# A two-step graph layer on one Trainium2 core: second step with sums put ahead of the mask, gathers issued singly, a finished tile's end moved, and small operations moved between engines

## The chip, the core and the metric

The kernel runs on one core of one Trainium2 chip. The core has TensorE (PE in the profile, its weight loads are PEld), VectorE (DVE), ScalarE (ACT), GpSimd (POOL) and SyncE (SP)[...] and 16 DMA engines. The metric is the device time of one execution, in microseconds (us); lower is better.

## The reference, cut to what matters

There are N = 3327 nodes with 256 features, padded to 26 tiles of 128 rows. `adj` is sparse: a row has about five entries, the diagonal among them.

```python
h = relu(layernorm(x))
R = (adj + I) / rowsum(adj + I)
Xf = Xa = h;  Z = 0
for n in (0, 1):
    q = Xa @ W1.T @ W2.T;  k = Xa @ W3.T              # 64 wide
    probs = softmax(q @ k.T)                          # 3327 x 3327
    A = probs, cut in each row to the fewest largest entries
        whose sum reaches 0.9, then divided by the row's sum
    Xf = R @ Xf
    Xa = A @ Xa
    Z = Z + Xf @ U1[n].T + Xa @ U2[n].T
out = x + layernorm(h + Z) * ln_g + ln_b
```

No row is sorted. A threshold is guessed for each row from passes of Relu and Sign over the exponentials; then the largest entries below the guess are found exactly, and the cut is placed among them. Had a guess failed, a flag would start a slow search at the end.

## The kernel before, in words

One program works through 26 tiles of 128 rows twice, `step` 0 and `step` 1. A tile's row block `e` is 128 x 3328 numbers in SBUF; step 1 has six such buffers, two of which lie in the former `x0` (the profile then writes `x` where it means such a block).

**What happens to one tile of step 1**, by generator, with its lines:

- `weights` (L580): query product (`pq`, L522), then products with the keys into PSUM (`pl`, L598) and the exponential into `e` (ACT, L602 to L608).
- `measured_twice` (L666): eight pieces. A row of small ACT operations (L618 to L673) makes a first guess; then a Relu pass over the whole block and a Sign pass (both `ja`, L631). Small operations on VectorE (L682, L683), ACT (L684 to L686) and GpSimd (L687 to L689) make a better guess; then a second Sign pass. L694 to L709 (GpSimd), L696, L697 (VectorE) and L699 to L711 (ACT) make the final guess, used by VectorE (L713, L714).
- `settle` (L722): VectorE writes `w`, the entries below the guess (L728), takes the 8 largest of each of 20 segments (L733, 20 MAX8), then the 48 largest of those (L740, L742, six rounds), finds the cut (L747 to L752), and masks `e` in place while it sums it (L762; the first and the last tile do it in two parts, L759). GpSimd multiplies two 48-wide rows (`cum`, L765) for a proof that VectorE ends (L769).
- `Sums` (L798): `turn` transposes a group of four 128 x 128 blocks of the masked `e` on TensorE (`pt`, L811), and ACT copies them out (`eT`, L813); `sum` multiplies them with `xw`, adding into PSUM `pa` (L825). A tile has seven groups. There are two `pt` buffers, three `eT` buffers and one `pa` buffer.
- `spread` (L1073): the sparse product, six 128-wide products (`pr`, L911) of the packed adjacency `ac` with gathered rows `xg`, and `s` on VectorE (L1086). `refetch` (L1092) loads `ac` and issues five gathers of 128 rows on GpSimd (L903), two buffers deep.
- `finish` (L934): VectorE adds the sums into `s` (L935) and takes mean and variance (L457, L458); GpSimd makes the scale (L464, L465, L943); ACT applies it (L950); GpSimd adds `bet` to the re-read `x` (L945), multiplies by `gam` (L951) and adds the two (L952); SP stores.
- `laws` (L548), once at the start of step 1: statistics of the query rows of tiles 3 to 25, ended by a power of 0.5 and eight more small GpSimd operations (L567 to L574).

**Their order is written out by hand.** Round `i` has seven slots. In each slot the letters of `PLAN[step][k]` let one generator advance by one piece: `m` measures tile i+1 and `n` ends the measuring that began in the round before; `d` settles tile i and `c` ends the settling of tile i-1, its mask (slot 0) and proof among it; `s` is `spread`, `w` and `q` are `weights`, `f` is `finish`, `g` the gathers, `l` the laws, `v` the final proof. `LAST` replaces the plan in the final rounds. Around the letters of a slot a `turn` (before them in step 1) and a `sum` (after them) are set. What is left of a generator runs at the round's end. Dependencies added at the end of the function then hold PE, ACT and VectorE, and in step 1 GpSimd, to this order: an engine that waits in one instruction holds up all that is written behind it.

Slot `k` of round `i` serves group `g = 7(i-1) + k - 4` in step 1, and `turn` runs two groups ahead. So a tile's sums begin in slot 4 of the round after its settling began, and its first transposes stand in slot 2, after its mask.

Of the kernel before, what the change touches and what calls it, by code (L numbers as in the profile page):

```python
# [9 lines left out]
F32 = mybir.dt.float32  # L10
# [334 lines left out]
def guess_graph_layer(ctx, tc, x, adj, w1t, w2t, w3t, u1t, u2t, ln_g, ln_b, out, flag):  # L345
# [60 lines left out]
    half = const.tile([P, 4], F32, tag="half", name="half")  # L406
    for k, c in enumerate((-0.5, 0.5, -1.0, -0.5)):
        G.memset(half[:, k : k + 1], c)
    halves = const.tile([P, NT], F32, tag="halves", name="halves")
    G.memset(halves, 0.5)  # L410
    law = const.tile([P, 7, NT], F32, tag="law", name="law")
    one = const.tile([P, 7], F32, tag="one", name="one")
    for k, c in enumerate((1.0, -1.0, 5.0e-4, SQG[1], SQK[1], math.log(10.0), LNY)):
        G.memset(one[:, k : k + 1], c)
    of_s = const.tile([P, 4], F32, tag="of_s", name="of_s")
    for k, c in enumerate((SQG[0], SQG[2], -SQK[0], -SQK[2])):
# [131 lines left out]
    def laws(ts):  # L548

        at = lambda k, a, b: law[:, k, a:b]  # L550
        few_of = [ts[h::2][n : n + 3] for n in range(0, len(ts), 3) for h in range(2)]
        for few in filter(len, few_of):
            pq = ps_t.tile([P, 4, P], F32, tag="pt", name="pq")
            pm = pq.rearrange("p a b -> p (a b)")[:, : 3 * (2 * DA + 2)].rearrange("p (t n) -> p t n", t=3)
            for k, t in enumerate(few):
                PE.matmul(pm[:, k, :], query_of(t), qm[query_at(t), 1, :], start=True, stop=True)
            wide = scan.tile([P, NP], F32, tag="w", name="wide")
            mq = wide[:, : 3 * (2 * DA + 2)].rearrange("p (t n) -> p t n", t=3)
            V.tensor_copy(mq[:, : len(few)], pm[:, : len(few)])
            V.tensor_copy(law[:, 2, few[0] : few[-1] + 1 : 2], mq[:, : len(few), DA])  # L560
            for k, t in enumerate(few):
                V.scalar_tensor_tensor(mq[:, k, : DA + 1], mq[:, k, : DA + 1], 1.0, mq[:, k, DA + 1 :],
                                       ALU.mult, ALU.mult, accum_out=at(1, t, t + 1))
            yield
        a, b = ts[0], ts[-1] + 1
        s, var, m = (at(k, a, b) for k in range(3))
        G.tensor_tensor(s, var, halves[:, a:b], ALU.pow)  # L567
        for k, c in ((3, SQG[0]), (4, SQG[2]), (5, -SQK[0]), (6, -SQK[2])):
            G.tensor_scalar(at(k, a, b), s, c, 1.0e-4, ALU.mult, ALU.add)
        G.tensor_tensor(at(4, a, b), at(4, a, b), var, ALU.add)  # L570
        G.tensor_tensor(at(4, a, b), at(4, a, b), m, ALU.add)
        G.tensor_scalar(m, m, 0.25, LNY - 0.25 * math.log(0.1 / N), ALU.mult, ALU.add)
        G.tensor_scalar(var, var, 0.125, None, ALU.mult)
        G.tensor_tensor(var, var, m, ALU.add)  # L574
# [91 lines left out]
    def measured_twice(r):  # L666
# [19 lines left out]
        S.activation(col(13), col(6), AF.Copy, scale=col(9))  # L686
        G.tensor_scalar(col(14), col(13), col(9), 0.25, ALU.add, ALU.mult)  # L687
        G.tensor_scalar(col(10), col(13), col(5), 1.0, ALU.mult, ALU.add)
        G.tensor_scalar(col(8), col(4), col(1), -1.0, ALU.mult, ALU.add)  # L689
        yield  # L690
        through(e, AF.Sign, col(13), -1.0, oa[:, 2:3])
        yield
# [8 lines left out]
        S.activation(col(3), d1, AF.Ln, scale=col(1), bias=con(2))  # L701
        S.activation(col(2), col(2), AF.Identity, scale=-1.0, bias=col(3))

        G.tensor_scalar(col(12), col(4), d1, col(1), ALU.subtract, ALU.mult)
        G.tensor_scalar(col(8), col(8), col(12), None, ALU.mult)
        G.tensor_scalar(col(12), col(12), col(12), 1.0e-12, ALU.mult, ALU.add)
        G.tensor_tensor(col(12), col(12), half[:, 2:3], ALU.pow)
        G.tensor_scalar(col(12), col(12), col(8), 0.7, ALU.mult, ALU.max)
        G.tensor_scalar(col(11), col(12), 1.5, col(11), ALU.min, ALU.mult)  # L709
        yield  # L710
# [11 lines left out]
    def settle(step, t, r):  # L722
# [38 lines left out]
        else:  # L761
            V.scalar_tensor_tensor(e, e, at(1), e, ALU.is_ge, ALU.mult, accum_out=ra)  # L762
        V.reciprocal(ra, ra)
        if step:
            G.tensor_tensor(cum[:, :n], dr[:, :n], b, ALU.mult)  # L765
        yield
        if not step:
            V.tensor_tensor(cum[:, :n], dr[:, :n], b, ALU.mult)
        V.tensor_reduce(at(2), cum[:, :n], AX.X, ALU.max)  # L769


# [103 lines left out]
    def gathered(t):  # L875
        oh = ohs.pop(t)
        ls, n = lists[:, t, :], LIST - DIRECT
        po = ps_t.tile([P, 4, P], F32, tag="pt", name="po")
        PE.matmul(po[:, 0, : n + 1], oh, ls[:, DIRECT:], start=True, stop=True)
        lo = small.tile([P, n], F32, tag="lo", name="lo", bufs=2)  # L880
        S.copy(lo, po[:, 0, :n])
        nth = small.tile([P, 1], F32, tag="nth", name="nth")
        S.activation(nth, po[:, 0, n : n + 1], AF.Identity, scale=-1.0, bias=part)
        yield
        of = small.tile([P, LIST], F32, tag="of", name="of", bufs=2)
        V.scalar_tensor_tensor(of[:, :n], place[:, :n], nth, lo, ALU.is_equal, ALU.mult, accum_out=nth)
        G.tensor_scalar(index[:, t, DIRECT:], nth, -1.0, float(NONE), ALU.mult, ALU.add)
        ac = adjp.tile([P, KT, P], F32, tag="ac", name="ac", bufs=2)
        nc.sync.dma_start(ac[:, KT - 1, :], adj[t, :, t, :])
        acs[t] = ac  # L890
        G.tensor_tensor(ac[:, KT - 1, :], ac[:, KT - 1, :], ident, ALU.add)
        rows = adj.rearrange("t p j r -> (t p j) r")
        for k in range(KT - 1):
            G.indirect_dma_start(out=ac[:, k, :], out_offset=None, in_=rows,  # L894
                                 in_offset=bass.IndirectOffsetOnAxis(ap=index[:, t, k : k + 1], axis=0),
                                 element_offset=t * P * NT * P)
        xgs[t] = fetched(bx, t, D + 1)

    def fetched(table, t, w):
        xg = adjp.tile([P, KT - 1, D + 1], F32, tag="xg", name="xg", bufs=2)  # L900
        rows = table.rearrange("p j d -> (p j) d")
        for k in range(KT - 1):
            G.indirect_dma_start(out=xg[:, k, :w], out_offset=None, in_=rows,  # L903
                                 in_offset=bass.IndirectOffsetOnAxis(ap=index[:, t, k : k + 1], axis=0))
        return xg


    def diffuse(ac, xg, own, w):
# [25 lines left out]
    def finish(t, y, pa, ra):  # L934
# [7 lines left out]
        nm = small.tile([P, 1], F32, tag="nm", name="nm")  # L942
        G.tensor_scalar(nm, mv[:, 0:1], rstd, -1.0, ALU.mult, ALU.mult)  # L943
        yield
        G.tensor_tensor(xr, xr, bet, ALU.add)  # L945
        if t == NT - 1:
            V.scalar_tensor_tensor(y, y, mv[:, 0:1], gam, ALU.subtract, ALU.mult)
            V.scalar_tensor_tensor(y, y, rstd, xr, ALU.mult, ALU.add)
        else:
            S.activation(y, y, AF.Identity, bias=nm, scale=rstd)  # L950
            G.tensor_tensor(y, y, gam, ALU.mult)  # L951
            G.tensor_tensor(y, y, xr, ALU.add)  # L952
        yield
        h = min(P, N - t * P)
        nc.sync.dma_start(out[t * P : t * P + h], y[:h])

# [135 lines left out]
    def refetch(t):  # L1092
        acs[t] = adjp.tile([P, KT, P], F32, tag="ac", name="ac", bufs=2)
        nc.sync.dma_start(acs[t].rearrange("p k r -> p (k r)"), cx[t])
        xgs[t] = fetched(vx, t, D)
        yield

# [1 line left out]


    PLAN = (("mdsssa", "mcdsssa", "edawwp", "msda", "mpdea", "gdwwq", "emgq"),
            ("llcmss", "lnms", "lwwnfd", "lcmdsssg", "fmswqdf", "llmdf", "lmwfd"))

    LAST = {NT - 1: ("cfss", "cn", "ndd", "sss", "fddddsf", "f", "f"), NT: ("cf", "", "", "", "ff", "fv", "f"),
            NT + 1: ("fv", "f", "", "", "f", "f", "f")}
    LATE = (1, 4)
    trace, begin = nc.cur_bb.bb.instructions, len(nc.cur_bb.bb.instructions)
    work = dict(m=none, d=none, f=none)  # L1110
    later = {}
    ordered = []
    for step in range(2):
        sums = Sums(step, live, xw if step else x0, AHEAD[step])

        for i in range(-1, NT + 2):
# [4 lines left out]
            if step == 1 and i == -1:  # L1121
# [11 lines left out]
                e=first_end(i - 2) if step == 0 and valid(i - 2) else none,  # L1133
                a=itertools.islice(lister, 9 if i else 3) if step == 0 else none,
                p=packed(i + 1) if step == 0 and i >= 0 and valid(i + 1) else none,
                g=none if not valid(i + 2 * step) else refetch(i + 2) if step else gathered(i),
                b=none, q=none, v=proof() if step and i == NT else work.get("v", none),
                l=laws(range(3, NT)) if step and i == -1 else none,
            )
            if i >= 0 and valid(i + 3):  # L1140
                later[step, i + 3] = weights(step, i + 3, live)
# [9 lines left out]
                work["w"] = begun[2]  # L1151
            if step == 0 and i < 1:
                work["b"] = itertools.islice(product, MADE if i else NT)
            if step == 1 and i == -1:
                work["g"] = itertools.chain(refetch(0), refetch(1))
            for k in range(PARTS):
                g = PARTS * (i - 1) + k - LATE[step]
                summing = valid(g // PARTS)
                if summing and step:
                    sums.turn(g, min(i, NT - 1))  # L1160
                for c in "bb" + (LAST.get(i, PLAN[1]) if step else PLAN[0])[k]:
                    next(work[c], None)
                if summing and not step:
                    sums.turn(g, min(i, NT - 1))
                if summing:
                    ended = sums.sum(g)
                    if ended and step == 0:
                        live["r", ended[0]] = ended[1]
                    elif ended:
                        work["f"] = finish(ended[0], live.pop(("f", ended[0])), *ended[1])  # L1170
            if step == 1 and i == -1:
                run(work["m"])
            if step == 0 and i == -1:
                G.memset(es[2][:, N:NP], 0.0)
            for c in "lcnwqsepgb" if step else "cmwqsepgb":
                run(work[c])
            if step == 0 and i == NT:
                moments(1, gsum)
# [52 lines left out]
```

## Time and profile before

| | us |
|---|---|
| median of three runs | 1431.23 (1426.26 to 1432.77) |
| the profiled execution | 1383.37 |
| its span | 1381.4 |
| granted TensorE clock, mean | 0.976 |
| busy: PE, DVE, ACT, POOL | 1271.7, 1207.6, 1109.1, 1022.8 |
| step 0, to about | 740 |
| start of step 1, to the mask of tile 1 | 740 to 811.51 |
| masks of tiles 1 to 23, start to start | 811.51 to 1300.58 |
| mask of tile 24 to the end | 1322.39 to 1381.4 |

The page gives busy time by engine, a strip of 40 slices, the chain of work that ended last, and the costliest groups of instructions; the trace behind it answers for single lines and stretches. Busy time counts the time in which an instruction was at work on an engine, so an engine can be 94% busy and still spend that time on a chain that passes through others. The profiled execution is one run, and it is shorter than the three timed ones.

### The profile page before, as it was taken

The numbers are of one execution on the slowest core, as the hardware profiler recorded it, in microseconds if no ns is written. First come the engines' busy times: TensorE is split into PE (matmuls) and PEld (weight loads), VectorE is DVE, ScalarE is ACT, GpSimd is POOL, SyncE is SP. The second block draws the span as 40 slices with busy tenths as digits, with TensorE's granted clock in tenths as the row PEclk, the third lists the DMA queues.
The fourth block names the chain that finished last, engine by engine and source line by source line (L and its number), as shares of the span: only waits on it lengthen the run. The fifth ranks groups of instructions, "written<-read, shape, count | busy, mean of one in ns | idle before, by whom it ended". The sixth has DMA issues, their size and how long they took to land.

```text
span 1381.4 us, 22149 instructions
## 1 busy us (share of the span) xinstructions
PE 1271.7 (92%) x6495; PEld 977.1 (71%) x6495; DVE 1207.6 (87%) x3595; ACT 1109.1 (80%) x2449; POOL 1022.8 (74%) x1374
## 2 busy tenths in 40 slices
PE   6898999999999999999997389999999999999885
PEld 5545777777877778787775267777776777777674
DVE  6878999999999999999944689999999999999992
ACT  5467888879888888888735689999999999999931
POOL 6225888888888888888843868888888888888832
PEclk9999999999999999999998589999999999999998
DMA  8884453545445453545331211212222221212100
GB/s 293 261 271 125 128 148 109 152 119 152 128 135 141 122 154 106 156 118 149 85 98 50 69 54 55 84 58 81 71 67 82 58 88 54 89 58 81 58 8 22
DMA packets 91202, 149.77 MB, mean 108 GB/s; under 512 B 15265, under 2 KB 58656, under 8 KB 91072
## 3 DMA queue, kind: packets, MB, share of 16 engines
q1 hardware_dynamic: 73616, 105.37, 24.4%
q0 software_dynamic: 16640, 42.69, 11.9%
q8 instruction: 54, 0.88, 0.3%
q14 instruction: 76, 0.62, 0.1%
q10 hardware_dynamic: 816, 0.20, 0.1%
HBM read 120.93 MB, written 27.28 MB: 107 GB/s over the span
## 4 chain that ended last, share of the span: by engine, by line
DVE 40%; PE 24%; ACT 17%; POOL 9%; DMA 4%; issue 4%; SPq 0%; POOLq 0%; DVEq 0%; ACTq 0%
ACT ja L631 11%; PE pa L825 9%; DVE e L762 9%; PE pl L598 5%; DVE cand L733 4%; DVE w L728 4%; DVE fm L847 4%; DVE bb L740 3%; DVE cand L742 3%; PE pt L811 3%; PE pz L988 3%; POOL xg L903 3%; POOL ac L894 2%; DVE x L762 2%; DMA at<-in_adj 2%
## 5 line engine op out<-in xcount | busy, mean ns | idle before, releaser
L825 PE MATMUL pa<-xw,eT 128*128 128x256 f32 x1352 | 330.8, 386 | 6.6 <-DVE s L935 6.5
L631 ACT ACTIVATE ja<-e,g 128x3328 uint8<-128x3328 f32 x106 | 325.8, 3074 | 0.1
L825 PE MATMUL pa<-x,eT 128*128 128x256 f32 x1352 | 323.1, 380 | 0.0
L825 PEld LDWEIGHTS pa<-xw,eT 128*128 128x128 f32 x1352 | 249.4, 191 | 67.9 <-issue 27.1
L825 PEld LDWEIGHTS pa<-x,eT 128*128 128x128 f32 x1352 | 243.7, 191 | 25.8
L733 DVE MAX8 cand<-w 128x8 f32<-128x168 f32 (+1 forms) x1040 | 251.5, 318 | 0.0
L813 ACT COPY eT<-pt 128x512 f32<-128x512 f32 (+1 forms) x364 | 201.9, 556 | 59.3 <-PE pt L811 58.8
L894 POOL DMA_INDIRECT ac<-in_adj,index x130 | 189.7, 1459 | 44.3 <-issue 30.5
L811 PE MATMUL pt<-ident,e 128*128 128x128 f32 x1144 | 180.1, 278 | 43.9 <-DVE e L762 21.9
L811 PEld LDWEIGHTS pt<-ident,e 128*128 128x128 f32 x1144 | 140.5, 144 | 90.2 <-issue 43.3
L903 POOL DMA_INDIRECT xg<-bx,index x130 | 158.0, 1216 | 39.2 <-issue 30.5
L728 DVE SCALAR_TENSOR_TENSOR w<-e,g 128x3328 f32<-128x3328 f32 x44 | 168.5, 3830 | 0.7
L903 POOL DMA_INDIRECT xg<-vx,index x130 | 130.9, 1007 | 45.6 <-issue 33.0
L762 DVE SCALAR_TENSOR_TENSOR e<-e,rec 128x3328 f32<-128x3328 f32 x40 | 153.6, 3840 | 0.6
L911 PE MATMUL pr<-xg,ac 128*128 128x257 f32 (+1 forms) x520 | 139.4, 392 | 11.3 <-DVE s L1086 11.1
L602 ACT ACTIVATE e<-pl 128x832 f32<-128x832 f32 x132 | 112.8, 859 | 30.2 <-PE pl L598 30.1
L911 PEld LDWEIGHTS pr<-xg,ac 128*128 128x128 f32 x520 | 94.0, 195 | 25.0 <-DVE s L1086 11.3
L740 DVE MAX8 bb<-cand 128x8 f32<-128x160 f32 x286 | 92.9, 325 | 6.4
L598 PE MATMUL pl<-after,qT 64*128 64x416 f32 x416 | 96.7, 559 | 0.6 <-ACT qT L527 0.6
L765 POOL TENSOR_TENSOR cum<-dr,bb 128x48 f32<-128x48 f32 x26 | 84.8, 3261 | 15.5 <-DVE rec L752 15.4
L951 POOL TENSOR_TENSOR s<-s,gam 128x256 f32<-128x256 f32 x25 | 92.6, 3703 | 3.2 <-ACT s L950 3.2
L598 PE MATMUL pl<-both,qT 64*128 64x416 f32 x416 | 90.1, 536 | 0.8 <-DVE both L1006 0.8
(257 smaller groups left out, 2200.0 us busy)
## 6 DMA issues: line engine op xcount, KB each, us to landing
at<-in_adj SPq DMA_DIRECT2D x102, 256.0 KB, 3.2
cx<-ac SPq DMA_DIRECT2D x26, 384.0 KB, 2.8
ac<-cx SPq DMA_DIRECT2D x26, 384.0 KB, 3.1
wide<-in_adj SPq DMA_DIRECT2D x10, 832.0 KB, 6.4
e<-in_adj SPq DMA_DIRECT2D x8, 832.0 KB, 5.1
bx<-e SPq DMA_DIRECT2D x26, 128.5 KB, 2.8
own<-bx SPq DMA_DIRECT2D x26, 128.5 KB, 3.2
x<-in_x SPq DMA_DIRECT2D x13, 256.0 KB, 5.4
```

Of the source, the lines that this page charges most:

```text
L598: PE.matmul(pl[:, a, :wd], qT[p, :], keys_of(step, a).rearrange("p a b -> p (a b)")[:, c : c + wd], start=True, stop=True)
L631: S.activation(ja, e, f, bias=guess, scale=sign, accum_out=total)
L728: V.scalar_tensor_tensor(w, e, col(16), e, ALU.is_lt, ALU.mult, accum_out=d2)
L733: V.max(cand[:, 8 * s : 8 * s + 8], w[:, s * SEG : min(NP, (s + 1) * SEG)])
L740: V.max(b8, cand)
L762: V.scalar_tensor_tensor(e, e, at(1), e, ALU.is_ge, ALU.mult, accum_out=ra)
L811: PE.transpose(pt[:, j, :], e[:, (j0 + j) * P : (j0 + j + 1) * P], ident)
L813: S.copy(eT[:, :w, :], pt[:, :w, :])
L825: PE.matmul(self.pa, eT[:, c - 4 * k, :], self.xa[:, j, :], start=c == 0, stop=c == NT - 1)
L894: G.indirect_dma_start(out=ac[:, k, :], out_offset=None, in_=rows, in_offset=bass.IndirectOffsetOnAxis(ap=index[:, t, k : k + 1], axis=0), ...
L903: G.indirect_dma_start(out=xg[:, k, :w], out_offset=None, in_=rows, in_offset=bass.IndirectOffsetOnAxis(ap=index[:, t, k : k + 1], axis=0))
L911: PE.matmul(pr[:, :w], ac[:, k, :], own if k == KT - 1 else xg[:, k, :w], start=k == 0, stop=k == KT - 1)
```

## The change

Step 0 keeps its instructions and their order. Line numbers above are those of the kernel before; the changed one is six to nine lines lower.

- **Sums and transposes.** In step 1 slot 1 runs two `sum`s and slot 2 none; the `turn` of slot 2 does two groups and the one of slot 3 none. Transposes of the first tile begin before its sums do.
- **Gathers.** `fetched` yields after each gather. One chain of all tiles' gathers is drawn on by each `g`; the new `OPEN` plans spread them over the first rounds. From round 4 on five stand together in slot 3.
- **Laws.** The power of 0.5 becomes Ln and Exp on ACT, and the last piece runs at the end of round 0.
- **Guess.** Three small GpSimd operations and a power become one operation and a reciprocal on VectorE; `spread` goes ahead of `measured` in slot 4.
- **Proof.** The 48-wide product goes from GpSimd to VectorE in step 1.
- **End of a tile.** `finish` has four pieces rather than five. The last, with the ACT scaling and the three GpSimd operations, runs in slot 2 of the next round, behind `w`; `bet` is added after `gam` is multiplied.
- **Last rounds.** `LAST` is reordered.

```diff
-        G.tensor_tensor(s, var, halves[:, a:b], ALU.pow)
+        S.activation(s, var, AF.Ln, bias=con(7))
+        S.activation(s, s, AF.Exp, scale=0.5)
...
-        G.tensor_scalar(col(8), col(4), col(1), -1.0, ALU.mult, ALU.add)
+        G.tensor_scalar(col(8), r["Z"], -0.1, col(4), ALU.mult, ALU.add)
...
-        G.tensor_scalar(col(12), col(4), d1, col(1), ALU.subtract, ALU.mult)
-        G.tensor_scalar(col(8), col(8), col(12), None, ALU.mult)
-        G.tensor_scalar(col(12), col(12), col(12), 1.0e-12, ALU.mult, ALU.add)
-        G.tensor_tensor(col(12), col(12), half[:, 2:3], ALU.pow)
+        V.tensor_scalar(col(12), col(4), d1, 1.0e-30, ALU.subtract, ALU.add)
+        V.reciprocal(col(12), col(12))
         G.tensor_scalar(col(12), col(12), col(8), 0.7, ALU.mult, ALU.max)
         G.tensor_scalar(col(11), col(12), 1.5, col(11), ALU.min, ALU.mult)
...
-        if step:
-            G.tensor_tensor(cum[:, :n], dr[:, :n], b, ALU.mult)
-        yield
-        if not step:
-            V.tensor_tensor(cum[:, :n], dr[:, :n], b, ALU.mult)
+        yield
+        V.tensor_tensor(cum[:, :n], dr[:, :n], b, ALU.mult)
...
-        G.tensor_tensor(xr, xr, bet, ALU.add)
         if t == NT - 1:
+            G.tensor_tensor(xr, xr, bet, ALU.add)
...
             S.activation(y, y, AF.Identity, bias=nm, scale=rstd)
             G.tensor_tensor(y, y, gam, ALU.mult)
+            G.tensor_tensor(xr, xr, bet, ALU.add)
             G.tensor_tensor(y, y, xr, ALU.add)
-        yield
...
-            ("llcmss", "lnms", "lwwnfd", "lcmdsssg", "fmswqdf", "llmdf", "lmwfd"))
-
-    LAST = {NT - 1: ("cfss", "cn", "ndd", "sss", "fddddsf", "f", "f"), NT: ("cf", "", "", "", "ff", "fv", "f"),
+            ("llcmss", "lnms", "lwwnfd", "lcmdsssggggg", "fsmwqdf", "llmdf", "lmwd"))
+
+    LAST = {NT - 1: ("cfss", "cn", "nd", "sss", "fdddddsf", "f", ""), NT: ("c", "", "", "ff", "ff", "fv", "f"),
             NT + 1: ("fv", "f", "", "", "f", "f", "f")}
+    OPEN = {-1: ("llcmss", "lnms", "lwwnfd", "lcmdsssggggg", "fmgswqdf", "llmdf", "lmwfdm"),
+            0: ("cmssggg", "nms", "wwnfd", "cmdsss", "fsmgwqdf", "mdf", "mwd"),
+            1: ("cmss", "nms", "wwnfd", "cmdsssggggg", "fsmwqdf", "mgdf", "mwd")}
+    OPEN[2] = OPEN[3] = OPEN[1]
+    fetching = itertools.chain(*(refetch(t) for t in range(NT)))
+    BLOCKS = ({}, {1: (0, 1), 2: ()})
...
-                if summing and step:
-                    sums.turn(g, min(i, NT - 1))
-                for c in "bb" + (LAST.get(i, PLAN[1]) if step else PLAN[0])[k]:
+                if step and valid((g + AHEAD[1]) // PARTS):
+                    sums.turn(g + (k == 2), min(i, NT - 1))
+                for c in "bb" + ({**OPEN, **LAST}.get(i, PLAN[1]) if step else PLAN[0])[k]:
                     next(work[c], None)
...
-                if summing:
-                    ended = sums.sum(g)
+                for n in BLOCKS[step].get(k, (0,)) if summing else ():
+                    ended = sums.sum(g + n)
...
+            if step and i < 1:
+                next(fetching)
-            for c in "lcnwqsepgb" if step else "cmwqsepgb":
+            for c in ("lcnwqsepb" if i > -1 else "cnwqsepb") if step else "cmwqsepgb":
                 run(work[c])
```

More of the change, by code (lines that the diff above doesn't have):

```diff
@@ L408, in guess_graph_layer @@
         G.memset(half[:, k : k + 1], c)
-    halves = const.tile([P, NT], F32, tag="halves", name="halves")
-    G.memset(halves, 0.5)
     law = const.tile([P, 7, NT], F32, tag="law", name="law")
-    one = const.tile([P, 7], F32, tag="one", name="one")
-    for k, c in enumerate((1.0, -1.0, 5.0e-4, SQG[1], SQK[1], math.log(10.0), LNY)):
+    one = const.tile([P, 8], F32, tag="one", name="one")
+    for k, c in enumerate((1.0, -1.0, 5.0e-4, SQG[1], SQK[1], math.log(10.0), LNY, 1.0e-12)):
         G.memset(one[:, k : k + 1], c)
@@ L896, in gathered @@
                                  element_offset=t * P * NT * P)
-        xgs[t] = fetched(bx, t, D + 1)
+        run(fetched(bx, t, D + 1))
     def fetched(table, t, w):
-        xg = adjp.tile([P, KT - 1, D + 1], F32, tag="xg", name="xg", bufs=2)
+        xgs[t] = xg = adjp.tile([P, KT - 1, D + 1], F32, tag="xg", name="xg", bufs=2)
         rows = table.rearrange("p j d -> (p j) d")
@@ L904, in fetched @@
                                  in_offset=bass.IndirectOffsetOnAxis(ap=index[:, t, k : k + 1], axis=0))
-        return xg
+            yield
     def diffuse(ac, xg, own, w):
@@ L1094, in refetch @@
         nc.sync.dma_start(acs[t].rearrange("p k r -> p (k r)"), cx[t])
-        xgs[t] = fetched(vx, t, D)
-        yield
+        yield from fetched(vx, t, D)
     PLAN = (("mdsssa", "mcdsssa", "edawwp", "msda", "mpdea", "gdwwq", "emgq"),
-            ("llcmss", "lnms", "lwwnfd", "lcmdsssg", "fmswqdf", "llmdf", "lmwfd"))
-    LAST = {NT - 1: ("cfss", "cn", "ndd", "sss", "fddddsf", "f", "f"), NT: ("cf", "", "", "", "ff", "fv", "f"),
+            ("llcmss", "lnms", "lwwnfd", "lcmdsssggggg", "fsmwqdf", "llmdf", "lmwd"))
+    LAST = {NT - 1: ("cfss", "cn", "nd", "sss", "fdddddsf", "f", ""), NT: ("c", "", "", "ff", "ff", "fv", "f"),
             NT + 1: ("fv", "f", "", "", "f", "f", "f")}
+    OPEN = {-1: ("llcmss", "lnms", "lwwnfd", "lcmdsssggggg", "fmgswqdf", "llmdf", "lmwfdm"),
[3 more added lines that the diff above has]
+    fetching = itertools.chain(*(refetch(t) for t in range(NT)))
     LATE = (1, 4)
+    BLOCKS = ({}, {1: (0, 1), 2: ()})
     trace, begin = nc.cur_bb.bb.instructions, len(nc.cur_bb.bb.instructions)
@@ L1135, in guess_graph_layer @@
                 p=packed(i + 1) if step == 0 and i >= 0 and valid(i + 1) else none,
-                g=none if not valid(i + 2 * step) else refetch(i + 2) if step else gathered(i),
+                g=fetching if step else gathered(i) if valid(i) else none,
                 b=none, q=none, v=proof() if step and i == NT else work.get("v", none),
-                l=laws(range(3, NT)) if step and i == -1 else none,
+                l=laws(range(3, NT)) if step and i == -1 else work["l"] if step and i == 0 else none,
             )
@@ L1153, in guess_graph_layer @@
                 work["b"] = itertools.islice(product, MADE if i else NT)
-            if step == 1 and i == -1:
-                work["g"] = itertools.chain(refetch(0), refetch(1))
             for k in range(PARTS):
```

## The prediction

> **What bounds the kernel now.** I read the busy times of all engines in stretches first.
>
> ```profile
> 300.00:400.00 100.00, 99.89 (x538) 79.17 (x534) 95.48 (x284) 83.62 (x209) 82.33 (x96) 1.00 0.46 134
> 760.00:780.00 20.00, 8.10 (x22) 4.35 (x22) 12.61 (x40) 12.81 (x25) 15.92 (x27) 0.59 0.22 61
> 780.00:800.00 20.00, 7.30 (x28) 4.49 (x25) 14.89 (x40) 14.59 (x28) 17.12 (x21) 0.59 0.24 70
> 1100.00:1200.00 100.00, 94.20 (x483) 72.94 (x482) 93.64 (x249) 94.52 (x194) 86.72 (x109) 1.00 0.23 68
> ```
>
> After the stretch and its length come busy us of PE, PEld, DVE, ACT, POOL, then the TensorE clock. Step 0 is TensorE's and the change leaves it alone. In step 1 PE, DVE and ACT all stand near 94%: none is full, so a chain through them sets the pace. The step's start is nearly empty. So I took the chain of waits for one period:
>
> ```profile
> 988.85 4.10 DVE e L762 x2
> 993.09 0.63 PE pt L811 x4
> 993.72 1.60 PE pl L598 x8
> 995.31 1.92 PE pa L825 x8
> 997.24 0.45 PE pt L811 x4
> 997.71 0.59 ACT eT L813
> 998.30 3.07 ACT ja L631 x2
> ...
> 1004.47 3.07 ACT ja L631 x2
> 1007.63 0.28 DVE g L696
> ...
> 1011.06 4.10 DVE x L762 x2
> ```
>
> Columns: start, duration, what. The mask (L762) frees one group of transposes; the next group waits behind 3.5 us of products, ACT's copy waits for it, and VectorE's L682 waits for ACT's Sign pass. From mask to mask: 22.21. Then GpSimd's timeline in the same period:
>
> ```profile
> 988.72 0.73 POOL L945 TENSOR_TENSOR xr<-xr,bet 128x256 f32<-128x256 f32 x1
> 989.41 4.11 POOL L951 TENSOR_TENSOR s<-s,gam 128x256 f32<-128x256 f32 x1
> 993.60 0.73 POOL L952 TENSOR_TENSOR s<-s,xr 128x256 f32<-128x256 f32 x1
> 994.28 3.66 POOL L765 TENSOR_TENSOR cum<-dr,bb 128x48 f32<-128x48 f32 x1
> ```
>
> L951 is as large as L945 but takes 4.11: it sits out VectorE's mask. The mask took 4.08 there and `w` (L728) 4.14; both took 3.69 around 811 to 816, where GpSimd was in no such operation when they started. At the step's start the chain names GpSimd:
>
> ```profile
> 763.64 4.01 POOL law L567
> ...
> 783.19 0.94 POOL xg L903
> ...
> 788.00 1.36 POOL g L709
> ```
>
> [...]
>
> **Part 1: the period of step 1.** Clock 0 is a mask's start. Before, from the VectorE and ACT timelines: mask and small operations 4.82; `w` to the first MAX8 4.42 (9.24); ten MAX8 2.35 (11.59); L935 0.48 with its end; 0.47 waiting for the Sign pass (12.54); L682, L683 and the step to ACT 0.50; ACT from L684 to its next pass (exponential and two copies among it) 2.46; pass and step to VectorE 3.28 (18.78); L696, L697 0.44; the last three rounds and the cut 3.00: 22.22. It closes.
>
> Edits, same clock:
>
> - `bet`, `gam` and their sum now run after `w`: ACT's scaling stands behind two exponentials and ends at about 8.3, so they fill 8.35 to 10.5 beside MAX8s. Mask 0.39 shorter, `w` 0.45 shorter. SP's store waits until 10.5 instead of 5; behind it stand `ac`, `xr` and the next tile's `own` and `s`, all needed some 20 us later.
> - The product on VectorE: 0.19 (L768, its twin in step 0) and 0.05 to the dependent reduction: +0.24. First MAX8 at 8.65, ten done at 11.00.
> - Slot 4 now has both `s` operations ahead of L682: 2 x 0.39, so L682 at 11.78. Behind it wait ACT's L684 and all that follows.
> - Sums ahead of the mask: PE does both groups at 3.85 to 4.9, ACT copies both at about 5.2 to 6.1, two exponentials and the scaling follow, and Sign ends near 11.4. VectorE's 0.47 and ACT's 0.54 of waiting go; what is late next is VectorE itself, by 0.4. PE no longer waits 1.16 for the mask, but waits for L935 to free `pa` (about 1.2), done at 11.5; its 14.4 us to the next transposes end at 25.9, beside the mask's end at 25.8: no loss.
> - ACT as before: 0.50 + 2.46 + 3.28: 18.02.
> - L696, L697, then the difference and the reciprocal (nearest rows 0.21 and 0.16; chained, +0.49): 0.93. Last rounds 3.00. **New period 21.95**, against 22.23 as the mean of 22: **-6** by the mask of tile 23. The three GpSimd operations and the power saved (1.9) lie beside VectorE and are worth nothing: `col(11)` is ready three us early. Gathers keep their place, end near 16.9 instead of 15, and are used over 20 us later.
>
> Bounds: if the two new operations fill waiting and `s` costs nothing, ACT's own load remains, 22.21 - 0.54 - 0.19 - 0.06 = 21.4 (-18). If the contention stays, 21.95 + 0.84 = 22.8 (+12).
>
> **Part 2: the start.** Before: final guess of tile 0, L711 at 763.68; ACT's L685 of tile 1 then waits to 777.57 for L674, behind the power (4.04), eight law operations (2.8) and five gathers (1.25 each with issue); L696 at 784.48 waits for five more; mask 0 at 787.90. After: the short guess gives 762.35 (-1.3); between L709's successor and L674 stands one gather. L674 sits out `w` (to 766.7), ends at 767.3, and ACT needs it at 772: no wait. Three gathers end at 771.3, one more at 774.8; the second Sign pass ends at 776.0, VectorE's rounds at 776.2; + 0.93 + 2.90: mask 0 at 780.1, **-7.8**. The laws follow a round later (two activations[...] and eight operations), under the masks of tile 0, with four us to spare. From mask 0 to mask 1 before took 23.61, with ACT waiting 2.39 and 0.71 for transposes; those now stand early, so the period of part 1 holds: another -1.6. Mask 1 at 802: **-9.5**. This part may lose 2 if gathers and `w` collide.
>
> **Part 3: the end.**
>
> ```profile
> 1349.45 0.60 ACT L950 ACTIVATE s<-s,nm,rstd 128x256 f32<-128x256 f32 x1 [7.16 <-POOL nm L943]
> 1350.58 0.66 PE L811 MATMUL pt<-ident,e 128*128 128x128 f32 x4 [3.12 <-ACT eT L813]
> ```
>
> In brackets: idle time before, and who ended it. ACT's copies of the last tile stood behind L950, which waited for statistics behind the last mask; the last tile's sums began 11.5 after that mask's start (1343.31). After: L950 comes behind two copies, PE ends tile 24 at +3.8, L935 comes at +5.4 behind six small operations, and the last sums begin at +6.1: -5.4. Ahead of that, `w` of tile 25 no longer waits 1.44 for L769's product: -1.3. **-6.7**. The seven groups (13.4) and the 13.2 after them are unchanged.
>
> **Sum.** -9.5 - 6.0 - 6.7 = -22.2: span 1381.4 to about 1359, execution 1383.4 to 1361. The median of the timed runs lies 47.9 above the profiled one; no view shows why, so I carry it over: 1431.2 - 22.2 = **1409**.
>
> **Rivals.**
>
> - *The period falls to ACT's load* (21.4): -12 more, 1397. For it: ACT's waits go. Against: L682 stands behind the whole of VectorE's chain. 0.12.
> - *The period stays at 22.2*: only the ends gain, 1415. For it: +0.24, +0.39 and +0.49 are close to the 0.84 and 0.47 gained; and if the 48 us are a slower TensorE, its 21.05 a period (22.21 less the 1.16) becomes the bound. 0.13.
> - *The edit misses its mark*: the moved GpSimd operations meet `w` or the mask after all; 22.8, so +12 against -16: 1427, within what can be measured. 0.10.
> - *Slower: GpSimd's three operations slow the MAX8s they now lie beside.* Up to 2.2 a tile on VectorE's chain: 24.1, +42 against -16: 1456. It decides from a period of 23.3, where (16 + 7)/22 is used up. Against: beside nine small GpSimd operations from 311.70 to 315.0, two lots of ten MAX8 took 2.44 and 2.40, as elsewhere. None of those operations was 256 wide. 0.10.
>
> **Numbers.** My forecast has 0.55. Differences under 0.5% (7 us) can't be told from none here. Faster: 0.55 + 0.12 + 0.13 = 0.80; same 0.10; slower 0.10. The range 1397 to 1427 reaches from the stronger case to the missed one.
>
> **What would show it.** Mask and `w` at 3.69 instead of 4.1; `gam` at 0.73; masks 21.95 apart; no wait of TensorE's transposes for the mask; VectorE waiting some 0.6 ahead of the second guess (L696) but not ahead of L682; mask 1 near 802; last sums 6 after the last mask. Wrong if MAX8 takes over 0.33, if GpSimd operations of 3 to 4 us remain beside masks, or if gathers hold up `pr`.

## The result, and the profile after

The changed kernel takes 1406.14 us (1405.30 to 1408.17, four runs) against 1429.20 (1426.26 to 1432.77, four runs): a ratio of 0.9838, 95% interval 0.9818 to 0.9858, or 23 us. The forecast was 1409, a gain of 22.2. In the changed kernel the lines named above stand one to six lower, not six to nine: the mask is L759, `w` L725, the final guess L693 to L708, `finish` L929 to L947, the gathers L897.

The two profiled executions can't be subtracted: 1383.37 before, 1405.77 after. Step 0, which the change leaves alone, runs in two rhythms. The profile of before fell in the quick one; that its timed runs were in the slow one is inferred from their times, since no trace of them exists. Hence the experiments below begin with a second profile of both kernels, both quick, which I call the second pair: spans 1383.2 and 1364.0. For one stretch of step 0, the view of busy times (start and end, length, then PE, PEld, DVE, ACT, POOL, TensorE clock, DMA share, GB/s) of the first profile after:

```profile
300.00:400.00 100.00, 93.59 (x492) 71.96 (x491) 87.01 (x267) 77.84 (x196) 64.65 (x87) 1.00 0.45 126
```

and of the second profile after:

```profile
300.00:400.00 100.00, 99.50 (x533) 78.74 (x532) 95.70 (x292) 84.31 (x210) 82.52 (x98) 1.00 0.47 135
```

The same kernel, the same clock, and 533 matmuls instead of 492 in 100 us. Step 0's last mask starts at 742.3 in the first and 704.0 in the second. Step 1's rhythm does not notice: its masks stand 21.85 apart in both.

The chain of waits through one period of step 1, first profile after (start, duration, what), lines left out at the dots:

```profile
976.76 3.71 DVE e L759 x2
...
988.22 0.39 DVE s L1080
988.61 0.13 DVE g L681
...
994.14 0.56 issue
...
994.76 0.28 DVE g L695
...
998.62 3.68 DVE e L759
```

Before, this chain ran through TensorE's transposes, ACT's copy and ACT's Sign pass to the second guess. Now the view keeps to VectorE from mask to mask; the 0.56 of "issue" is its wait for ACT's second Sign pass, which the view doesn't name. The mask starts 21.86 after the one before and takes 3.69, as `w` does. GpSimd's timeline of the same period:

```profile
978.63 2.04 POOL L673 TENSOR_SCALAR g<-g,law 128x1 f32<-128x1 f32 x1 [2.93 <-ACT g L672]
...
985.25 0.73 POOL L945 TENSOR_TENSOR s<-s,gam 128x256 f32<-128x256 f32 x1 [4.28 <-ACT s L944]
...
997.24 0.31 POOL L706 TENSOR_SCALAR g<-g 128x1 f32<-128x1 f32 x1
```

`gam` (L945 here) takes 0.73 where it took 4.11. Only L673 still sits out a mask, until 980.67, and nobody waits for it. The last line matters most: GpSimd's share of the final guess ends at 997.55, 1.07 ahead of the next mask.

Stretch by stretch, from the starts of the masks in both second profiles:

| | before | after | gain | forecast |
|---|---|---|---|---|
| last mask of step 0 to mask 0 | 86.56 | 78.78 | -7.78 | -7.8 |
| mask 0 to mask 1 | 23.41 | 21.81 | -1.60 | -1.6 |
| masks 1 to 23 | 489.03 | 482.41 | -6.62 | -6.0 |
| mask 23 to 24 | 21.80 | 24.94 | +3.14 | -0.1 |
| mask 24 to 25 | 20.93 | 19.51 | -1.42 | -1.3 |
| mask 25 to the end | 38.06 | 32.59 | -5.47 | -5.4 |

The sum is -19.75; the first masks of step 0 differ by 0.6, which leaves the 19.2 between the spans. The timed runs of this pair differ by 23: the profile of before lies 2.3 under the median of its timed runs, that of after at the median, and no view shows why. The first row is not steady either: in the two first profiles this stretch took 85.95 and 81.47. The 2.7 by which 81.47 exceeds 78.78 are lost ahead of tile 0's final guess (L695 comes 61.64 instead of 58.96 after step 0's last mask).

### The profile page after: what moved, and what is told of

Read it like the earlier page. It is cut to its first block, busy times and chain, and to the rows that moved or that the text cites. A ratio compares the mean times of both kernels' runs of the same rounds, so it can differ in the third digit from the quotient of the medians.

```text
span 1404.0 us, 22095 instructions
## 1 busy us (share of the span) xinstructions
PE 1275.7 (91%) x6495; PEld 976.9 (70%) x6495; DVE 1195.0 (85%) x3673; ACT 1105.3 (79%) x2451; POOL 795.3 (57%) x1243
## 4 chain that ended last, share of the span: by engine, by line
PE 43%; DVE 40%; ACT 11%; issue 4%; DMA 1%; POOL 1%; SPq 0%; another core or an unknown queue 0%; DVEq 0%; ACTq 0%; POOLq 0%
PE pa L819 18%; DVE cand L730 8%; DVE w L725 7%; PE pt L805 6%; DVE e L759 5%; PE pr L905 4%; PE pl L597 4%; DVE cand L739 3%; ACT ja L630 3%; DVE bb L737 3%; PE pz L982 3%; PE pz L918 3%; DVE x L759 2%; ACT eT L807 2%; PE pk L1023 1%
## 5 line engine op out<-in xcount | busy, mean ns | idle before, releaser
L819 PE MATMUL pa<-xw,eT 128*128 128x256 f32 x1352 | 323.6, 384 | 27.4 <-DVE s L929 26.2
L805 PE MATMUL pt<-ident,e 128*128 128x128 f32 x1144 | 176.1, 276 | 18.2 <-DVE e L756 9.1
L897 POOL DMA_INDIRECT xg<-bx,index x130 | 156.6, 1205 | 45.2 <-issue 31.5
L725 DVE SCALAR_TENSOR_TENSOR w<-e,g 128x3328 f32<-128x3328 f32 x44 | 162.1, 3684 | 0.7
L888 POOL DMA_INDIRECT ac<-in_adj,index x130 | 130.3, 1002 | 44.5 <-issue 29.6
L897 POOL DMA_INDIRECT xg<-vx,index x130 | 129.5, 996 | 38.6 <-issue 38.6
L759 DVE SCALAR_TENSOR_TENSOR e<-e,rec 128x3328 f32<-128x3328 f32 x40 | 147.5, 3688 | 0.6
L673 POOL TENSOR_SCALAR g<-g,law 128x1 f32<-128x1 f32 x23 | 46.4, 2017 | 67.4 <-ACT g L672 67.4
L922 POOL TENSOR_TENSOR sv<-sv,x 128x256 f32<-128x256 f32 x26 | 19.8, 763 | 109.9 <-ACT sv L921 109.9
```

The lines of the kernel that those rows point to most:

```text
L725: V.scalar_tensor_tensor(w, e, col(16), e, ALU.is_lt, ALU.mult, accum_out=d2)
L805: PE.transpose(pt[:, j, :], e[:, (j0 + j) * P : (j0 + j + 1) * P], ident)
L819: PE.matmul(self.pa, eT[:, c - 4 * k, :], self.xa[:, j, :], start=c == 0, stop=c == NT - 1)
```

## The experiments

Each ratio is an estimate, with its interval, of a run's time over that of the kernel before on the same chip (medians 1387 to 1389 us). It differs from the ratio of the medians by up to 0.15%, which is 2 us. Gains and losses in us are differences of these ratios, unless medians are given; 1% is 14 us. Where two intervals overlap, the masks of the traces say more than the times. "Period" is the usual distance of masks in step 1.

| run | period | ratio (95%) |
|---|---|---|
| before_again | 22.22 | one run |
| after_again | 21.85 | 0.9835 (0.9813 to 0.9856) |
| sums_only | 21.80 | 0.9946 (0.9928 to 0.9965) |
| end_only | 23.54 | 1.0204 (1.0183 to 1.0224) |
| guess_back | 23.55 | 1.0137 (1.0115 to 1.0159) |
| sums_back | 22.24 | 0.9918 (0.9893 to 0.9944) |
| end_back | 22.01 | 0.9854 (0.9834 to 0.9874) |
| s_back | 21.67 | 0.9827 (0.9804 to 0.9851) |
| eight_first | 21.57 | 0.9811 (0.9792 to 0.9830) |
| product_back | 21.62 | 0.9793 (0.9771 to 0.9814) |
| start_back | 21.85 | 0.9898 (0.9877 to 0.9920) |
| tail_back | 21.85 | 0.9879 (0.9858 to 0.9901) |

**The two kernels once more.** No edit.

> The kernel before, unchanged, profiled once more. My account: the 48 us between the profiled execution (1383) and the timed ones (1431) lie in step 0, which can run in a quicker or a slower rhythm with the same instructions; the new profile runs the slower one, as the changed kernel's did, step 0 ends near 775 instead of 733, masks of step 1 stand 22.2 apart as before, and the span is near 1427. Rival: the profile of this kernel is always 48 us short, whatever the run: span near 1381 again, with step 0 done near 733.

> The changed kernel, unchanged, on the chip on which the variants ran. My account: step 0 takes 40 us less here for every kernel, step 1 is as in its first profile: masks 21.86 apart, last mask to the end 32.6, time about 1363, that is -24 us against the kernel before on the same chip (1387). Rival (step 0's rhythm carries over into step 1): another period.

Of the two accounts of the 48 us, the rival held for the kernel before: 1385.04, span 1383.2, step 0 as quick as in its first profile. But its eight timed runs were now quick as well (1387.31), and so was the changed kernel (1365.71, where the 1406 stood). So the 40 us belong neither to the change nor to profiling. The changed kernel's two traces place 38.3 of them ahead of step 0's last mask; the kernel before has a trace of the quick rhythm alone, and its two medians (1429.20 and 1387.31) lie as far apart. What decides the rhythm is open; all twelve later profiles ran the quick one. The change is worth 23 us in either rhythm.

**One part alone: the moved end.** Before, with the last piece of `finish` behind `w`:

```diff
-        G.tensor_tensor(xr, xr, bet, ALU.add)
         if t == NT - 1:
+            G.tensor_tensor(xr, xr, bet, ALU.add)
...
+            G.tensor_tensor(xr, xr, bet, ALU.add)
             G.tensor_tensor(y, y, xr, ALU.add)
-        yield
...
-"lmwfd"
+"lmwd"
```

> The kernel before with one part of the change: the last piece of `finish` (ACT scaling and three GpSimd operations) behind `w`. My account: mask and `w` at 3.69, MAX8 still at 0.317; the chain still runs through the transposes, ACT's Sign pass and the second guess, so only the mask's 0.39 counts: masks 21.8 apart, -8.6 us, about 1420. Rival A (contention is worth nothing, the sums alone brought the gain): 22.2, 1429. Rival B (mask and `w` both count): 21.4, -18, 1411.

All three accounts failed: 23.54, and 28 us slower than before. Mask and `w` are at 3.69, as wanted. Its chain of waits, from one mask (974.28) to past the next (997.85):

```profile
974.43 3.70 POOL g L708
...
978.24 0.31 POOL g L709
...
978.58 0.29 ACT g L711
...
985.06 3.07 ACT ja L631 x2
...
988.15 0.23 DVE g L682
...
998.00 3.70 POOL g L708
```

L708 works on 128 x 1 numbers; its neighbour L709 takes 0.31. Started 0.15 after the mask, it sits out the whole mask. ACT's exponential L711 waits for it, the next tile's Relu pass stands behind that, and so on round to L708, which meets the next mask again. The three operations of `finish` now run at 10 to 13 us into the period, ahead of the gathers, and push GpSimd's queue back: the first gather starts 12.8 after the mask, and L694 starts 1.0 after VectorE's L696. In the kernel before, the chain L694 to L709 ended some 0.1 short of the mask, here of the one at 1011.06:

```profile
1010.61 0.34 POOL L709 TENSOR_SCALAR g<-g 128x1 f32<-128x1 f32 x1
```

**One part alone: the sums.** Before, with two groups of sums in slot 1 and their transposes together:

```diff
+    BLOCKS = ({}, {1: (0, 1), 2: ()})
...
-                    sums.turn(g, min(i, NT - 1))
+                    sums.turn(g + (k == 2), min(i, NT - 1))
...
-                if summing:
-                    ended = sums.sum(g)
+                for n in BLOCKS[step].get(k, (0,)) if summing else ():
+                    ended = sums.sum(g + n)
```

> The kernel before with one part of the change: two groups of sums in slot 1 and their transposes together, ahead of the mask. My account: ACT's Sign pass ends in time, VectorE's wait of 0.47 ahead of the second guess goes, mask and `w` stay at 4.1: masks 21.75 apart, -10 us, 1419. Rival (TensorE waiting for its accumulator takes the gain back): above 22.0, -4 us or less. Neither alone reaches the period of the changed kernel (21.86) by the same way: here L728 and L762 stay long.

21.80 and -7.5 us, with mask and `w` still at 4.1: near what was expected.

**The sums undone.** The changed kernel with `BLOCKS = ({}, {})` and `turn(g, ...)`:

> The changed kernel with its sums and transposes one group to a slot, as before (the new early transposes of the first tile kept). My account: the Sign pass ends at 12.1 after the mask's start instead of 11.35, VectorE waits for it, masks 22.3 apart, +9 us against the changed kernel. The final guess is short, so no GpSimd operation meets the mask: not 23.5. Rival (the moved end alone brought the period down): 21.86 as in the changed kernel.

22.24 and +11.5 us. In ACT's timeline the first Sign pass ends at 948.31, 12.11 after the mask's start (936.20). VectorE's timeline has the second guess at once behind it:

```profile
948.34 0.21 DVE L681 TENSOR_SCALAR g<-oa,g 128x1 f32<-128x1 f32 x1
```

This is the wait that was worked out. The sums are worth 0.39 a period. The guess is short and ends some 2 us ahead of the mask; only L673 meets the mask, as in the changed kernel.

**The guess undone.** The changed kernel with the three GpSimd operations and the power back:

```diff
-        G.tensor_scalar(col(8), r["Z"], -0.1, col(4), ALU.mult, ALU.add)
+        G.tensor_scalar(col(8), col(4), col(1), -1.0, ALU.mult, ALU.add)
...
-        V.tensor_scalar(col(12), col(4), d1, 1.0e-30, ALU.subtract, ALU.add)
-        V.reciprocal(col(12), col(12))
+        G.tensor_scalar(col(12), col(4), d1, col(1), ALU.subtract, ALU.mult)
+        G.tensor_scalar(col(8), col(8), col(12), None, ALU.mult)
+        G.tensor_scalar(col(12), col(12), col(12), 1.0e-12, ALU.mult, ALU.add)
+        G.tensor_tensor(col(12), col(12), half[:, 2:3], ALU.pow)
```

> The changed kernel with the final guess as before: three GpSimd operations and a power instead of one operation and a reciprocal on VectorE. The prediction's working (these operations are worth nothing on GpSimd, 0.49 on VectorE): masks 21.4 to 21.5 apart, -9 us against the changed kernel. The account that the run with the end moved alone forced on me: GpSimd's chain of eight small operations starts about 1 us after L696's twin, the mask comes 3.4 us after it, so the fifth or sixth operation meets the mask and sits it out (3.70); ACT's next Relu pass waits for it, and the period is the loop through it: 23.5, +36 us, slower than the kernel before.

23.55 and +42 us. In its chain, L707 (the twin of L708; mask at 968.10) does the same:

```profile
968.78 3.17 POOL g L707
...
972.40 0.29 ACT g L710
```

**The end undone.** The changed kernel with the last piece of `finish` in slot 6 again, `bet` first (the reverse of the edit above; the plans of rounds 1 to 3 likewise).

> The changed kernel with the last piece of `finish` in slot 6 again, `bet` first, ahead of the mask. My account: mask 4.08 and `w` 4.14 again, both on VectorE's chain, which sets the period: 21.86 + 0.84 = 22.7, +18 us. Rival A (only the mask counts, as the prediction worked it for the kernel before): 22.25, +9. Rival B (contention is worth nothing): 21.86.

A period of 22.01: between the accounts, Rival B the least far off. The +2.6 us can't be told from none (the medians are 1365.64 and 1365.71). VectorE's timeline and GpSimd's:

```profile
979.05 3.84 DVE L759 SCALAR_TENSOR_TENSOR e<-e,rec 128x3328 f32<-128x3328 f32 x1
```

```profile
978.69 0.73 POOL L945 TENSOR_TENSOR s<-s,gam 128x256 f32<-128x256 f32 x1 [1.03 <-ACT s L944]
979.49 4.00 POOL L946 TENSOR_TENSOR s<-s,xr 128x256 f32<-128x256 f32 x1
```

With the guess short, these operations come earlier: only the last 0.37 of L945 overlaps the mask, which grows by 0.15, and `w` meets none that is running and stays at 3.69. L946 starts inside the mask and sits it out, as L674 (3.50) does with `w`, without harm. So in these traces the one that is first goes on: VectorE's operation grew where a 256-wide GpSimd operation was already running, and one that GpSimd started later ended 0.60 behind VectorE's (L946). Not every running operation slows VectorE, though: in the kernel before, the 23-wide power of `laws` ran from 763.61 to 767.65, and the `w` that started at 764.32 took 3.69.

**What bounds the changed kernel next.** `spread`'s operation behind the second guess again (`"fsmwqdf"` to `"fmswqdf"`, in the opening rounds too):

> The changed kernel with the second guess ahead of `spread`'s operation on VectorE again (slot 4). The prediction's working: VectorE's chain loses 0.39, the period falls to 21.47 (ACT's load is 21.4), -8 us, 1398. A second account, from the changed kernel's trace: mask to freed accumulator 11.51, TensorE 14.40 to the next transposes, 7.30 to the end of the Sign pass, 10.15 to the mask are a loop of two periods, 43.36, so the period can't fall under 21.68: -4 us, 1402. Rival: the order of the two does not matter, 21.86, 1406.

21.67: the second account to 0.01. The chain now reaches over two periods; from the freed accumulator to the second guess of the next tile:

```profile
924.79 0.39 DVE s L929
...
925.22 1.99 PE pa L819 x8
...
936.33 3.45 PE pa L819 x16
939.78 0.87 PE pt L805 x8
...
943.88 3.06 ACT ja L630 x2
...
946.97 0.22 DVE g L681
```

925.22 to 939.78 is TensorE's unbroken run. From mask 1 to mask 23 it took 480.68 instead of 482.42, where 0.18 a period would give 4: one period of 23.58, explained with the next run, took back the rest. The ratio's 1 us can't be told from none.

**Eight MAX8 ahead of the sums' end.**

```diff
-            if s in (NSEG // 2 - 1, NSEG - 1):
+            if s in (NSEG // 2 - (3 if step else 1), NSEG - 1):
```

> The changed kernel with eight of the twenty MAX8 of step 1 ahead of the sums' last addition instead of ten (twelve after it). A test of the loop of two periods: VectorE's way from the mask to the freed accumulator and to the second guess is 0.48 shorter, so VectorE's loop is 21.38 and the loop through TensorE (43.36 - 0.48) / 2 = 21.44; ACT's load is 21.4. Masks 21.4 to 21.5 apart, -9 us against the changed kernel, which makes it the fastest so far. Rival (the moved MAX8 end later than the second Sign pass, or GpSimd's gathers hold its L686 longer): 21.86 or more.

21.57, not 21.44, and -3.3 us (masks 1 to 23: 478.32). The chain of waits keeps to ACT for nearly the whole period. ACT is busy 20.91 of one 21.57, and of its waits the timeline shows one, 0.19 for L696; the rest are steps from one instruction to the next. ACT's load, put at 21.4, was 0.15 too low. And one period of 23.55 cost 2; GpSimd's timeline there (mask at 845.19):

```profile
844.90 0.30 POOL L705 TENSOR_SCALAR g<-g 128x1 f32<-128x1 f32 x1
845.30 3.74 POOL L706 TENSOR_SCALAR g<-g 128x1 f32<-128x1 f32 x1
```

The trap of the run with the end alone, once: in that round the plan issues a sixth gather, and the mask comes earlier. `s_back` and `product_back` have it in the same place, with this operation at 3.74 too. The changed kernel misses it there by 0.2: L706 starts 0.19 ahead of the mask of tile 3 (848.33 in the second profile) and takes 0.30.

**The product undone.**

```diff
         V.reciprocal(ra, ra)
+        if step:
+            G.tensor_tensor(cum[:, :n], dr[:, :n], b, ALU.mult)
         yield
-        V.tensor_tensor(cum[:, :n], dr[:, :n], b, ALU.mult)
+        if not step:
+            V.tensor_tensor(cum[:, :n], dr[:, :n], b, ALU.mult)
```

> The changed kernel with the proof's 48-wide product on GpSimd in step 1. My account: VectorE's loop loses 0.24 and is 21.62, the loop of two periods is (43.36 - 0.24) / 2 = 21.56: masks 21.6 apart, -5 us. Rival: GpSimd's product starts as the mask does, so that the mask or GpSimd's next operation is held (mask over 3.7 or a product of 3 to 4 us): 21.86 or more.

21.62 and -5.9 us, as expected. This part of the change costs what the prediction charged (0.24). GpSimd's product starts 0.05 behind the mask and takes 3.76, as the rival had it, but nobody waits for it. At 1359.8 it is, with the kernel of eight MAX8 (1359.8), the fastest here; both beat the changed kernel's 1365.7.

**The start undone, the tail undone.** The start: the laws' power on GpSimd and their last piece in round -1, ten gathers in round -1 (`run(fetching, 5)` at its end). The tail: the `LAST` of before.

> The changed kernel with the start of step 1 as before: the laws' power on GpSimd and all ten first gathers in round -1. My account: the first mask comes 7 to 8 us later (88.6 after step 0's last mask instead of 81), nothing else moves: masks 21.86 apart, +7.5 us. Rival (the gain of the start comes from the short final guess alone): +0 to +2.

> The changed kernel with the last rounds' plan as before. My account: ACT's copies of the last tile stand behind the scaling of an earlier tile again, the last mask to the end takes 38.1 instead of 32.6: +5.5 us. Rival (the order of the last rounds is hidden behind TensorE's seven groups): 32.6, no change.

The start: mask 0 comes 87.45 after step 0's last mask instead of 78.78, +8.7, and the time is 9.0 longer. The tail: 39.64 instead of 32.59, +7.05, and the time 5.4 longer. Both as expected, a little larger. Laws and gathers were undone together, so their shares are not shown; the laws' two activations took 0.30 and 0.22 (L565 and L566, first profile after).

## Why the prediction was right

**The steps that held.** The place of every stage in the period: first MAX8 8.64 after the mask (8.65 forecast), L681 at 11.77 (11.78), L695 at 18.00 (18.02); only the last part was 3.86 instead of 3.93. The period is 21.85 (21.95). That GpSimd's three operations would cost nothing beside MAX8 was my estimate, from smaller ones; MAX8 stayed at 0.317 on average with the three 256-wide ones beside it, so the rival in which GpSimd slows it is out. The start and the end held to 0.1 in each of their two terms; part of that is luck, since the first stretch alone differs by 0.6 between the two profiles of the kernel before.

**"The three GpSimd operations and the power saved (1.9) lie beside VectorE and are worth nothing"** is the step that failed. They are worth 1.7 a period (23.55 less 21.85), more than any other part: with them the moved end makes the kernel slower. I noted for each operation of `finish` whether it meets a mask, but never asked it for the guess, which ended just ahead of it. The answer stood in the first trace of before, whose GpSimd timeline has, at a mask of 1033.28:

```profile
1033.43 3.70 POOL L708 TENSOR_SCALAR g<-g 128x1 f32<-128x1 f32 x1
```

That period took 23.06 instead of 22.22, and I averaged it in; the last line of the start's chain, L709 at 1.36 beside the first mask, is of the same kind. The sum came out because both edits were in, and that was luck: the working would have taken the moved end alone for a gain.

**"Mask 0.39 shorter, `w` 0.45 shorter"**, credited to the moved end, was seen, but the credit was misplaced: beside the other edits the move is worth 0.16 a period (22.01 less 21.85), and little or nothing in time, since the short guess alone brings GpSimd's operations out of `w`. The bound "if the contention stays, 22.8" was wrong for the same reason. The terms of a period don't add: sums alone -0.42, end alone +1.32, all together -0.37.

**Of the rivals**, a fall to ACT's load was stopped by VectorE, as argued; behind VectorE stood first a loop through TensorE of two periods, 21.67, which I had called "no loss" (true at 21.95), and then ACT at 21.57. The rivals' evidence counted nine small operations beside the MAX8s; there are ten, which changes nothing. A period unchanged, and an edit that misses its mark, are refuted by the mask starts.

**Mask 23 to 24**, put at -0.1, lost 1.9 in the first profile and 3.1 in the second. With sums early and no products with the keys left in this round, TensorE stands idle and comes back slow. PE's timeline in the second profile before and in the second after, and the busy times of after's stretch:

```profile
1314.56 1.99 PE L825 MATMUL pa<-xw,eT 128*128 128x256 f32 x8 [2.49 <-DVE s L935]
```

```profile
1298.75 3.78 PE L819 MATMUL pa<-xw,eT 128*128 128x256 f32 x8 [3.94 <-DVE s L929]
```

```profile
1298.70:1302.70 4.00, 3.95 (x10) 3.13 (x11) 3.90 (x18) 0.97 (x3) 1.00 (x4) 0.50 0.23 66
```

Eight matmuls take 3.78 instead of 1.99, at a granted clock of 0.50, behind a wait of 3.94 instead of 2.49. Other runs below show that the length of the wait alone does not decide. The clock is not the whole loss: in `s_back`, where eight matmuls behind a wait of 3.82 took 2.00, the stretch still took 22.73.

**One odd period**, 23.65 in the changed kernel, costs 1.8: GpSimd issues nothing for 2.64 ahead of a gather (1014.63 in the second profile), and L686, behind five gathers, comes late for L695. Its cause was not tried. It hides a miss: the usual period is 0.10 shorter than forecast, 2.2 over 22 periods, and the odd one takes most of it back, so masks 1 to 23 agree with the forecast better than the working did.

**The 47.9 us**, carried over unexplained, were rightly kept out of the sum: some 40 of them are step 0's rhythm; the rest is not explained.

## What to carry to other kernels

When a change shortens one chain, list every small operation that ends just ahead of the long one on an engine seen to collide with it, and say by how much; 0.1 us of margin decided here between 22.2 and 23.5 a period. Here one of 128 x 1 numbers sat out the whole long one, 3.70 instead of 0.3. Look in the old trace for single instances that are ten times as long as their neighbours; one stood there. And test parts alone as well as undone: the end alone said +28 us, the end undone 0.16 a period, and only both together tell that it does harm alone and none in company.

## What the runs showed of the hardware

- A GpSimd operation of 128 x 1 numbers takes 0.3, but took 3.70 when it started 0.15 after a mask of 3.70 (L708 in `end_only`, 974.43). One that started within 0.01 of a mask ran on in its 0.57 (L706 in `guess_back`, 968.11). On VectorE's side, 0.37 of overlap with a 256-wide operation already running cost a mask 0.15 (`end_back`, 979.05). Beside MAX8 neither grew: in the first profile after, the three 256-wide operations from 985.25 on took 0.73 each, and the ten MAX8 from 985.40 on took 2.44. Why mask and MAX8 differ in this is not shown.
- Behind waits of TensorE of 3.94 (second profile after), 3.65 (`eight_first`), 3.42 (`product_back`) and 3.19 (`guess_back`) the clock was 0.50, with eight matmuls at 3.78. They took 2.00 behind one of 3.82 (`s_back`), 2.64 behind one of 3.94 (`start_back`), and 2.71 behind one of only 2.56 (`sums_back`). So the length of the wait alone does not decide; what does is not shown. In step 1 of the two first profiles the stretches at half clock, but the last, lasted 10.24, 17.07, 17.07 and 3.41 before, and 10.24, 20.48 and 3.41 after.
- VectorE kept to the written order: in the first profile before, L696 (784.48) waited 6.41 for GpSimd's L687, and the L740 behind it, whose input had been done since 778.07, started only at 784.92.
- Step 0 runs the same instructions in two rhythms, its last mask at 704.0 or 742.3 in the changed kernel; the timed runs suggest the same of the kernel before.
